# An attention, attention and recurrence kernel: the first image loaded ahead of the parameters, extra products at the start, projections of the first image in pairs, and the last image's blocks in another order

## The chip, the cores and the metric

The kernel runs on one core of a Trainium2 chip. A core has TensorE (PE: matrix products, and PEld for its weight loads), VectorE (DVE), ScalarE (ACT), GpSimd (POOL) and SyncE (SP), which here only issues DMAs. The engines run side by side, each taking its own instructions in order, and wait for each other through semaphores. The metric is the device time of one execution in microseconds; less is better.

## The reference

The input is x, four images of 128 channels and 64 x 64 = 4096 positions, in fp32. Two layers follow.

```
# layer 0, per image
g   = group_norm(x, 32 groups)
vg  = sigmoid(conv_bn(g, Wvg, svg, bvg));  v, gate = split(vg)
q   = conv_bn(g, Wq, sq, bq) * 64 ** -0.5          # 64 x 4096
k   = conv_bn(g, Wk, sk, bk)                        # 64 x 4096
o   = v @ softmax(q.T @ k).T * gate                 # 128 x 4096
x   = x + conv_bn(o, Wp, sp, bp)
# layer 1, per image, t = x as 4096 tokens of 128
h   = layer_norm(t);  qt = h @ W;  t = t + softmax(qt @ qt.T) @ h
# then over all images
wx  = batch_norm(layer_norm(t) @ Wf.T)
y_n = sigmoid(wx_n + y_(n-1) @ V.T)                 # a scan over the tokens
out = t + y
```

conv_bn is a product with a 1 x 1 weight, then a scale and a bias per channel.

## The kernel before, in words

**Sizes.** An image's 4096 positions are eight blocks of 512 (`QB`). An fp32 product shows in the trace as two TensorE instructions; products whose operands have 64 rows run two at a time in the upper and lower half of the array.

**Layer 0** (`attention`, lines 184 to 240, with the callbacks of `layer0`). For each query block n it steps through 16 steps p. A step makes two 64-row score products (L223), one exponential on ScalarE over 1024 columns (L225), an addition on VectorE that collects the softmax's denominators (L230, L232), and, two steps late, the products with the values (L403). After each step one piece of other work is taken from the queue `ahead` or, when that is empty, from `pending`.

**Projections** (`prepare`, lines 289 to 386). The image lies in one tile `xg`. It is loaded in four pieces on SP's queue (L303). `stats` takes the statistics of 512 columns at a time (L307); `mean` and `variance` aggregate (L310) and average over groups with two tiny products (L312, L322), and `inv_sqrt` (L131, L132) runs on GpSimd. `normalise` (L328) works in place. `queries_keys` (L335) makes q and k of 512 positions, moved out of PSUM by VectorE (L339), ScalarE (L343, the copy of q for the lower half of the array) and VectorE again (L347). `values` (L355) makes four value tiles, followed by L360, a tanh on ScalarE (L364) and L365, which together are the sigmoid. `gate` (L370) makes the gate in the same way (L371, L374) and writes it over the normalised image. `chunks` holds four lists, each of two normalisings, two `queries_keys` and two `values`, for chunk i and chunk i + 4; step p of the first query block needs the keys of chunk p // 4 and of that plus four.

For the first image, the statistics, the norm and the first list run before the attention starts (L732); the three other lists and eight gates go into `ahead` (L735), and `need` (L739) takes more of them out when a step needs its keys. For later images all this lies in `ahead` during the layer 1 of the image before.

**Residuals.** When a query block is done, `finish` loads its piece of x (L419), adds a bias on GpSimd (L420) and puts `sums`, `denominators`, `projection` and `tokens` on `pending`. `move` (L257) turns a tile: a 32 x 32 transpose on VectorE (L261), a store to DRAM (L264) and four loads back (L266).

**Layer 1** (`layer1`, lines 475 to 716). Its scores are symmetric, so block n is multiplied only with blocks a from n down to 0; in the order 6, 7, 5, 4, ... 0. Each pair (n, a) is two steps of scores (L672) and exponentials (L678). The products with h (L539, `direct`) come two steps late. For a < n the exponentials are also turned (L683, then 16 DMAs, L710), and `reversed_products` (L552) gives block a its part. `quarter` (L500) saves part of the diagonal pair. `count` finishes a block when it has all its parts: `finish` puts `tokens` (the division, L604 to L610, and a layer norm), `result`, `turn` and `inputs` (L635 to L639) on `pending`. For the last image the pair (1, 0) isn't turned; instead block 0 makes the pair (0, 1) itself, after (0, 0).

**The end.** Batch norm's gain and bias are made (L791 to L796), six dummy products put the banks in order (L787), and 43 steps of the scan follow (L823, L827), each with a sigmoid on ScalarE. Sigmoid isn't in the table that serves Exp and Tanh here. Ahead of that, a sigmoid of one column (L764) is written, whose result no one reads.

**What sets the order.** The program is written as one long list, and a planner then gives each engine its order: it takes what its own estimates show as ready, earlier in the list first. So work can run long before its place in the list: the sigmoid of L764, near the end of the list, runs at 7.3 us. `tc.keep_in_program_order` keeps an instruction at its place.

**The start.** Weights (`w`, 512 KB), per-channel columns (`par`), and four rows repeated over all partitions (`bc`) are loaded on ScalarE's queue (L73 to L81). VectorE multiplies the value and output weights by two of these rows (L122, L123) and halves two columns (L127). Masks are made on GpSimd and VectorE.

## Time and profile before

| | us |
|---|---|
| median of 4 runs (lowest to highest) | 3069.51 (3068.19 to 3070.48) |
| the profiled execution | 3068.22 |
| its span in the trace | 3066.5 |
| first statistics (L307) start | 6.28 |
| group statistics aggregated (L310) from | 15.37 |
| first normalising (L328) | 18.81 |
| first exponential (L225) | 30.12 |
| TensorE without a pause from | 31.2 |
| last product of the attention (L539) ends | 2965.0 |
| last input of the scan (L639) done | 2978.1 |
| scan's last sigmoids (L827) end | 3040.3 |

The trace is of one execution. Busy time is time in which an engine ran an instruction; a busy TensorE isn't always at full clock, and the granted clock is given by stretches (1.00 is full, 0.50 half). Until the first closing that it records the trace shows 1.00, so at the start the clock is read from the instructions' lengths. The chain of waits follows the work back from the last instruction: each piece is what the next one waited for. An instruction's line (L335) is its line in the kernel before.

### The profile page before, as it was taken

The page shows a single profiled execution, that of the slowest core. Times are in us where ns is not written, and L with a number is a line of the kernel's source. Part 1 is how long each engine was busy: PE and PEld are TensorE (multiplying, and loading weights), DVE is VectorE, ACT ScalarE, POOL GpSimd, SP SyncE. Part 2 cuts the span into 40 slices and gives each one's busy share as a digit, 9 for nine tenths or more (in the row PEclk, how much of TensorE's full clock was granted, in tenths as well). Part 3 has the DMA queues.
Part 4 walks back from the last instruction along what each step waited for, and adds up shares of the span by engine and source line. Part 5 has one row for each costly group of instructions (what it writes and reads, how often), then busy time and mean ns, then how long its engine had stood idle before and what let it go on. Part 6 is the DMA issues. An engine that isn't in the chain of part 4 may idle for free.

```text
span 3066.5 us, 32642 instructions
## 1 busy us (share of the span) xinstructions
PE 2999.6 (98%) x10834; PEld 1377.9 (45%) x10834; DVE 1881.1 (61%) x3160; ACT 1154.3 (38%) x2148; POOL 148.6 (5%) x187
## 2 busy tenths in 40 slices
PE   7999999999999999999999999999999999999995
PEld 3444444444444444444444444444444444444443
DVE  6666666655666666655566666655566666455556
ACT  3444433333344443333344443333333444323334
POOL 0000000000000000000000000000000000000000
PEclk9999999999999999999999999999999999999998
DMA  1011143433111123333311113333321112543333
GB/s 52 28 56 56 42 115 86 99 92 93 52 56 55 42 79 97 93 96 91 84 48 60 40 49 109 90 96 93 94 61 56 42 50 93 138 102 92 99 113 157
DMA packets 233171, 241.17 MB, mean 79 GB/s; under 512 B 88480, under 2 KB 144288, under 8 KB 231968
## 3 DMA queue, kind: packets, MB, share of 16 engines
q1 hardware_dynamic: 231984, 238.18, 27.8%
q8 instruction: 89, 1.46, 0.2%
q10 hardware_dynamic: 1008, 0.79, 0.1%
q14 instruction: 90, 0.74, 0.1%
HBM read 65.80 MB, written 56.62 MB: 40 GB/s over the span
## 4 chain that ended last, share of the span: by engine, by line
PE 95%; DVE 3%; ACT 1%; POOL 0%; DMA 0%; issue 0%; ACTq 0%; SPq 0%; DVEq 0%; POOLq 0%
PE o L403 29%; PE o L539 16%; PE ps L223 15%; PE ps L672 14%; PE ot L552 12%; PE m L252 1%; PE m L635 1%; PE mq L497 1%; PE ps L505 1%; PE mp L335 1%; PE mp L370 1%; PE mp L355 1%; DVE t2s L837 1%; DVE ps_r L810 1%; PE m L630 1%; PE m L608 0%
## 5 line engine op out<-in xcount | busy, mean ns | idle before, releaser
L403 PE MATMUL o<-e,nxt 64*128 64x512 f32 x4096 | 964.4, 589 | 0.0
L225 ACT ACTIVATE e<-ps 128x1024 f32<-128x1024 f32 x512 | 521.6, 1025 | 678.0 <-PE ps L223 653.4
L232 DVE TENSOR_TENSOR acc<-acc,e 128x1024 f32<-128x1024 f32 x448 | 548.1, 1223 | 236.8 <-ACT e L225 221.1
L403 PEld LDWEIGHTS o<-e,nxt 64*128 64x128 f32 x4096 | 399.3, 187 | 483.2 <-issue 475.4
L678 ACT ACTIVATE e<-ps,shift 128x512 f32<-128x512 f32 x516 | 350.4, 683 | 670.4 <-PE ps L672 506.1
L539 PE MATMUL o<-e,h 128*128 128x512 f32 x1160 | 539.5, 592 | 0.0
L223 PE MATMUL ps<-nxt 64*128 64x512 f32 x2048 | 536.2, 597 | 2.2 <-ACT e L225 2.2
L672 PE MATMUL ps<-qt 128*128 128x512 f32 x1032 | 490.9, 595 | 2.9 <-ACT qt L498 2.7
L552 PE MATMUL ot<-tt,h 128*128 128x512 f32 x888 | 399.6, 593 | 0.2 <-issue 0.2
L683 DVE STREAM_TRANSPOSE dd<-e 128x512 f32<-128x512 f32 x444 | 286.9, 687 | 85.7 <-ACT e L678 80.2
L539 PEld LDWEIGHTS o<-e,h 128*128 128x128 f32 x1160 | 218.3, 190 | 266.4 <-issue 261.9
L223 PEld LDWEIGHTS ps<-nxt 64*128 64x128 f32 x2048 | 194.5, 187 | 231.4 <-issue 158.6
L672 PEld LDWEIGHTS ps<-qt 128*128 128x128 f32 x1032 | 187.9, 190 | 213.0 <-issue 188.0
L552 PEld LDWEIGHTS ot<-tt,h 128*128 128x128 f32 x888 | 167.9, 190 | 210.0 <-issue 207.3
L557 DVE TENSOR_REDUCE slots<-tt 128x4 f32<-128x2048 f32 x111 | 250.7, 2259 | 8.8 <-DMA tt<-dd 8.2
L566 DVE TENSOR_TENSOR oacc<-oacc,ot 128x512 f32<-128x512 f32 x87 | 59.6, 685 | 188.2 <-PE ot L552 188.1
L131 POOL TENSOR_SCALAR rstd<-mv 128x4 f32<-128x4 f32 x64 | 14.6, 228 | 2432.0 <-DVE mv L277 2432.0
L678 ACT ACTIVATION_READ_ACCUMULATOR e<-ps,shift 128x1 f32 x516 | 101.2, 196 | 0.0
L457 DVE SCALAR_TENSOR_TENSOR t<-yt,rinv,t 128x128 f32<-128x128 f32 x128 | 36.6, 347 | 72.9 <-DMA yt<-turn_d 68.0
L420 POOL TENSOR_SCALAR xb<-xb,bpc 128x512 f32<-128x512 f32 x32 | 61.1, 1909 | 320.2 <-DMA xb<-in_x_dram 320.2
L132 POOL TENSOR_TENSOR rstd<-rstd,mhalf 128x4 f32<-128x4 f32 x64 | 66.4, 1038 | 5.3
L280 DVE TENSOR_SCALAR h<-t,mv,rstd 128x128 f32<-128x128 f32 x128 | 35.7, 342 | 47.1 <-POOL rstd L132 47.1
(160 smaller groups left out, 1657.6 us busy)
## 6 DMA issues: line engine op xcount, KB each, us to landing
tt<-dd SPq DMA_DIRECT2D x1776, 64.0 KB, 2.0
turn_d<-d SPq DMA_DIRECT2D x96, 256.0 KB, 2.0
t_d<-t SPq DMA_DIRECT2D x63, 256.0 KB, 2.0
nxt<-in_x_dram SPq DMA_DIRECT2D x16, 512.0 KB, 6.1
xb<-in_x_dram SPq DMA_DIRECT2D x32, 256.0 KB, 2.9
t<-turn_d SPq DMA_DIRECT2D x128, 64.0 KB, 2.0
yt<-turn_d SPq DMA_DIRECT2D x128, 64.0 KB, 2.0
qt<-turn_d SPq DMA_DIRECT2D x128, 64.0 KB, 2.1
```

Of the source, the lines that this page charges most:

```text
L132: nc.gpsimd.tensor_tensor(dst, dst, mhalf[:, :n], ALU.pow)
L223: nc.tensor.matmul(ps[:, h, :], lhsT=lhsT, rhs=rhs, start=True, stop=True)
L225: nc.scalar.activation(e, ps, AF.Exp, scale=scale)
L232: nc.vector.tensor_tensor(acc, acc, e, ALU.add)
L403: nc.tensor.matmul(o[r], lhsT=v[rs, p + h * PAIRS, :], rhs=e[rs, h, :], start=(p == 0 and h == 0), stop=(p == PAIRS - 1 and h == 1),)
L420: nc.gpsimd.tensor_scalar(xb, xb, bpc, None, ALU.add)
L539: nc.tensor.matmul(o, lhsT=h[:, NQ * a + 2 * i + half, :], rhs=e[:, half, :], start=(a == order(n)[0] and i == 0 and half == 0), stop=(a = ...
L552: nc.tensor.matmul(ot, lhsT=h[:, NQ * n + j, :], rhs=t[:, :, j, :, :].rearrange("q p k j -> q k p j"), start=(j == 0), stop=(j == NQ - 1),)
L557: nc.vector.tensor_reduce(slots[:, bass.ts(n, NQ), a], t.rearrange("q p b k j -> q b p (k j)"), AX.XY, ALU.add,)
L672: nc.tensor.matmul(ps[:, half, :], lhsT=qt[:, bass.ts(at, P)], rhs=qt[:, bass.ts(n, QB)], start=True, stop=True,)
L678: nc.scalar.activation(e[:, half, :], ps[:, half, :], AF.Exp, bias=shift, accum_out=slots[:, at, n : n + 1],)
L683: nc.vector.transpose(d.rearrange("q f b k j -> q k b f j")[:, 2 * i + half], e[:, half, :].rearrange("q (b f j) -> q b f j", b=NQ, f=NQ),)
```

## The change

- The loads of weights and rows move from ScalarE's queue to SP's, into a function `load` that is called after the first image's loads are issued; the rows' order changes. The first image is loaded in eight pieces instead of four.
- The scalings of L122, L123 and L127 move into `scales`, called after the group norm of the first image.
- `warm` makes products that no one reads: three of 512 columns ahead of the statistics, and one of 256 columns each after `mean` and `variance`.
- For the first image, each `queries_keys` and the `values` of the same chunk become one piece of work, and so do two gates; gates alternate between two PSUM pools. `need` counts four pieces a chunk instead of six.
- The first turn (L261) and the sigmoid of L764 are kept at their place in the list, and so are the extra products.
- In the last image's layer 1, block 0 makes the pair (0, 1) first and (0, 0) after; block 1 counts one part more, which it gets when the exponentials of (0, 1) are written.

```diff
--- before.py
+++ after.py
@@ -70,15 +70,20 @@
     wx_d = dram.tile([B, C, N], F32, name="wx_d")
 
     w = const.tile([P, 8 * P], F32, name="w")
-    nc.scalar.dma_start(w, wts)
     w_q, w_k, w_v, w_g, w_p, w_a, w_f, v_t = (w[:, bass.ts(i, P)] for i in range(8))
     par = const.tile([P, 8], F32, name="par")
-    nc.scalar.dma_start(par, cols)
     bpc = const.tile([P, 1], F32, name="bpc")
-    nc.scalar.dma_start(bpc, rows[3:4, :].rearrange("a p -> p a"))
     bc = const.tile([P, 4, P], F32, name="bc")
-    for i in range(4):
-        nc.scalar.dma_start(bc[:, i, :], rows[i, :].partition_broadcast(P))
+
+    def load():
+
+        nc.sync.dma_start(w, wts)
+        nc.sync.dma_start(par, cols)
+        for i in (0, 1):
+            nc.sync.dma_start(bc[:, i, :], rows[i, :].partition_broadcast(P))
+        nc.sync.dma_start(bpc, rows[3:4, :].rearrange("a p -> p a"))
+        for i in (2, 3):
+            nc.sync.dma_start(bc[:, i, :], rows[i, :].partition_broadcast(P))
 
     def col(i):
         return par[:, i : i + 1]
@@ -118,13 +123,15 @@
     nc.gpsimd.memset(ones, 1.0)
     shift = const.tile([P, 1], F32, name="shift")
     nc.gpsimd.memset(shift, -SHIFT)
-
-    nc.vector.tensor_mul(w_v, w_v, bc[:, 0, :])
-    nc.vector.tensor_mul(w_p, w_p, bc[:, 2, :])
     w_vs, w_ps = w_v, w_p
-
     par2 = const.tile([P, 2], F32, name="par2")
-    nc.vector.tensor_scalar(par2, par[:, SG : BG + 1], 0.5, None, ALU.mult)
+
+    def scales():
+
+        nc.vector.tensor_mul(w_v, w_v, bc[:, 0, :])
+        nc.vector.tensor_mul(w_p, w_p, bc[:, 2, :])
+
+        nc.vector.tensor_scalar(par2, par[:, SG : BG + 1], 0.5, None, ALU.mult)
 
     def inv_sqrt(dst, var, eps):
         n = dst.shape[1]
@@ -136,6 +143,7 @@
         tc, x, out, t_d, t2_d, wxs_d, turn_d,
         dict(qk=w[:, DQ : DQ + P], vs=w_vs, g=w_g, ps=w_ps, a=w_a, f=w_f, vt=v_t),
         col, par, par2, bpc, bc, ident, gavg, quart, own, shift, inv_sqrt, par_ok,
+        load, scales,
     )
 
 
@@ -157,7 +165,7 @@
 
 def fast(
     tc, x, out, t_d, t2_d, wxs_d, turn_d, wt, col, par, par2, bpc, bc, ident, gavg, quart,
-    own, shift, inv_sqrt, par_ok,
+    own, shift, inv_sqrt, par_ok, load, scales,
 ):
     nc = tc.nc
     keep_ctx = ExitStack()
@@ -258,7 +266,9 @@
 
             nonlocal n_moves
             d = work.tile([P, 4, NQ, 32], F32, tag="d", name="d", bufs=2)
-            nc.vector.transpose(d.rearrange("q a j i -> q j a i"), blocks)
+            turned = nc.vector.transpose(d.rearrange("q a j i -> q j a i"), blocks)
+            if n_moves == 0:
+                tc.keep_in_program_order(turned)
             via = turn_d[n_moves % len(turn_d)]
             n_moves += 1
             nc.sync.dma_start(via, d)
@@ -289,6 +299,13 @@
         def quarters(t):
             return [t[:, j, :].rearrange("q (p i) -> q p i", p=4) for j in range(NQ)]
 
+        def both(first, second):
+            def run():
+                first()
+                second()
+
+            return run
+
         def prepare(b, bank):
 
 
@@ -299,8 +316,10 @@
             mv = stat.tile([P, 2], F32, tag="gmv", name="gmv", bufs=2)
             dev = stat.tile([P, 3], F32, tag="gdev", name="gdev", bufs=2)
             s6 = stat.tile([P, 8, 6], F32, tag="gs6", name="gs6", bufs=1)
-            for i in range(4):
-                nc.sync.dma_start(xg[:, bass.ts(i, N // 4)], x[b, :, bass.ts(i, N // 4)])
+            pieces = 8 if b == 0 else 4
+            for i in range(pieces):
+                cs = bass.ts(i, N // pieces)
+                nc.sync.dma_start(xg[:, cs], x[b, :, cs])
 
             def stats(i):
                 for j in range(2 * i, 2 * i + 2):
@@ -366,7 +385,7 @@
 
             def gate(ch):
                 cs = bass.ts(ch, 512)
-                m = bank(True)
+                m = bank(ch % 2 == 0)
                 nc.tensor.matmul(m, lhsT=wt["g"], rhs=xg[:, cs], start=True, stop=True)
                 nc.scalar.activation(
                     xg[:, cs], m, AF.Tanh, bias=par2[:, 1:2], scale=par2[:, 0:1]
@@ -383,6 +402,10 @@
                     + [partial(values, c) for c in pair]
                 )
             gates = [partial(gate, c) for c in range(8)]
+            if b == 0:
+
+                chunks[1:] = [[*c[:2], both(c[2], c[4]), both(c[3], c[5])] for c in chunks[1:]]
+                gates = [both(*gates[i : i + 2]) for i in range(0, 8, 2)]
             return (xg, q, k, v), norm, chunks, gates
 
         def layer0(b, gate, q, k, v, need):
@@ -528,7 +551,7 @@
             def order(n):
 
 
-                return [0, 1] if b == B - 1 and n == 0 else list(range(n, -1, -1))
+                return [1, 0] if b == B - 1 and n == 0 else list(range(n, -1, -1))
 
             def turns(n, a):
                 return a < n and not (b == B - 1 and n == 1)
@@ -573,7 +596,7 @@
 
 
                 parts[n] += 1
-                if parts[n] == NB - (b == B - 1 and n < 2):
+                if parts[n] == NB - (b == B - 1 and n == 0):
                     finish(n)
 
             def finish(n):
@@ -696,8 +719,10 @@
                         clock += 1
                         if len(fifo) > LAG:
                             direct()
-                            if a == n and i == 0:
+                            if a == order(n)[0] and i == 0:
                                 direct()
+                        if a > n and i == 1:
+                            count(a)
                         if turned and turned[0][0] <= clock:
                             reversed_products()
                         if pending:
@@ -729,7 +754,26 @@
             return own_bank(spare)
 
         parts0, norm, chunks, gates = prepare(0, first_bank)
-        for work_ in norm + chunks[0]:
+        load()
+
+        def warm(cols):
+
+            m = ps_o.tile([P, QB], F32, tag="o", name="warm")
+            tc.keep_in_program_order(
+                nc.tensor.matmul(
+                    m[:, :cols], lhsT=ident, rhs=parts0[0][:, :cols], start=True, stop=True
+                )
+            )
+
+        for _ in range(3):
+            warm(QB)
+        for work_ in norm[:-2]:
+            work_()
+        for work_ in norm[-2:]:
+            work_()
+            warm(QB // 2)
+        scales()
+        for work_ in chunks[0]:
             work_()
         started.append(True)
         ahead.extend(sum(chunks[1:], []) + gates)
@@ -739,7 +783,7 @@
         def need(n, p):
 
             if n == 0:
-                while p // 4 > 0 and n_ahead - len(ahead) < 6 * (p // 4):
+                while p // 4 > 0 and n_ahead - len(ahead) < 4 * (p // 4):
                     ahead.popleft()()
 
         for b in range(B):
@@ -761,7 +805,7 @@
         flush()
 
 
-        nc.scalar.activation(first_y, shift, AF.Sigmoid)
+        tc.keep_in_program_order(nc.scalar.activation(first_y, shift, AF.Sigmoid))
         ok = big.tile([P, 2, 2 * B * NT], F32, tag="oacc", name="ok")
         nc.vector.tensor_scalar(ok[:, 0, :], den_all, DEN_LO, None, ALU.is_ge)
         nc.vector.tensor_scalar(ok[:, 1, :], den_all, DEN_HI, None, ALU.is_le)
```

## The prediction, made before the result was known

> **What bounds the kernel now.** First the page: TensorE is busy nearly throughout, so the long middle is worth nothing to an edit that removes no TensorE work. Only a place where TensorE stands still, runs at half clock, or pays for switching can give time back.
>
> ```profile
> PE 2999.6 (98%) x10834; PEld 1377.9 (45%) x10834; DVE 1881.1 (61%) x3160; ACT 1154.3 (38%) x2148; POOL 148.6 (5%) x187
> ```
>
> Second, the chain of waits of the start (start, length, what). The reader is to see that the first image's group norm is reached only at 15.37, by way of a residual block (`xb`), its bias add and its turn (L261), which the planner hoisted from work due 60 us later; that the first projections (L335) take 0.94 us an instruction; that a table load stands right before the first exponential; and that the next scores (L223 x4) take 2.08 us.
>
> ```profile
> 8.34 4.56 DMA xb<-in_x_dram
> 12.99 1.64 POOL xb L420
> 14.66 0.71 DVE d L261
> 15.37 0.26 DVE gmv L310
> ...
> 18.81 0.56 DVE nxt L328
> 19.41 3.78 PE pp L335 x4
> 23.19 1.36 PE po L355 x8
> ...
> 28.18 0.63 ACT nxt L364
> 28.83 1.28 ACT L225
> 30.12 1.03 ACT e L225
> 31.20 2.08 PE ps L223 x4
> ```
>
> Third, the image's loads (L303): the first image in two stretches, then the second image, which has the queues to itself. Three loads go out at 0.8 to 1.7 us, but the fourth only at 8.0, and lands 4.3 later, at 12.3. The second image's four go out within 1.4 us, and the last lands by 397.4 + 6.8 = 404.2, 8.1 us after the first issue.
>
> ```profile
> L303 SPq DMA_DIRECT2D nxt<-in_x_dram x3: 393/427/432, 0.8 to 1.7; - x3
> L303 SPq DMA_DIRECT2D nxt<-in_x_dram x1: 328/328/328, 8.0 to 8.0; - x1
> L303 SPq DMA_DIRECT2D nxt<-in_x_dram x4: 351/430/431, 396.1 to 397.4; - x4
> DMA to landing us min/median/max: 4.1/5.4/6.8
> ```
>
> Fourth, the clock, in a table by stretches (length, busy time of PE, PEld, DVE, ACT and POOL, granted clock, DMA). TensorE was idle from 28.99 to 31.20, and the gate closed at about 30.7 for 3.5 us.
>
> ```profile
> 31.00:31.50 0.50, 0.30 (x2) 0.30 (x4) 0.00 (x0) 0.50 (x2) 0.00 (x0) 0.50 0.00 0
> ```
>
> Fifth, the chain of the first query block and of the end. A gate product (L370) costs 1.05 for two instructions and the four score instructions after it 1.06, where undisturbed ones take 0.86 each: 0.39 for going from half-height to full-height weights and back. At the end, the last block's sum (L566) waits behind the layer norm (L280) of the block before it.
>
> ```profile
> 76.65 1.05 PE po L370 x2
> 77.70 1.06 PE ps L223 x4
> 78.76 1.72 PE o L403 x8
> ...
> 2964.24 1.05 POOL rstd L132
> 2965.32 0.04 DVE h L280
> 2965.36 0.22 issue
> 2965.58 0.85 DVE h L280 x3
> 2966.43 0.61 DVE oacc L566
> ```
>
> **The change, part by part.**
>
> (1) **Image first, parameters behind it on SP, first turn held back.** With ACT issuing nothing, I take the second image's pace: last piece at 0.8 + 8.1 = 8.9, one L307 (0.68) to 9.6. Eight pieces instead of four let the statistics run along (8 x 0.6 = 4.8 us of VectorE, begun near 4.2). Aggregation starts at 9.6 instead of 15.37: -5.7. Worst: the last piece lands at 12.3 as now, statistics done at 13.0, -2.4; best, nearer to the 7.5 of the third load now: -6.3. The chain L310 to L328 (3.5 us) is unchanged, so normalising starts near 13.1. SP now issues eight loads and seven parameter loads: 15 x 0.43 = 6.5 us, during which data flow, so w (512 KB at 1.33 us by the second image's pace) lands near 10.2 and the four `bc` rows by about 12.5. In `scales` the product of w_p with the third of them may stand on VectorE ahead of the normalising, and all the projections wait behind it; cover is the 3.5 us of the group norm's chain. `bc` lands up to 7.4 us after issue now; issued at 6.4 that is 13.8: cost 0.7; each further us costs one. I take 0.2. The residual block, queued on SP behind the parameters, isn't needed before the first block ends. The held turn (0.71) then runs on VectorE, which is busy 44.3 of 76 us in the first block. Sum -5.5.
>
> (2) **Extra products.** Three of 512 columns are six instructions, cold 0.94 each: 5.7 us from the first piece's landing (about 4.2) to 9.9, when the mean's product is due at 10.0; uncovered they would cost up to 0.3. The two half ones stand in gaps of the group-norm chain. Gain, if the first projections run warm: the four L335 take 1.7 instead of 3.78 and L355 0.89 instead of 1.36, but VectorE is busy normalising meanwhile and waited for PE only 0.23 (L339) and 0.54 (L360): at most 0.8. Is the gate still open at 13.7? The stretch from 27.3 to 30.7 held 1.7 us of products, and the gate closed. Between 10 and 13.4 the extra and group-norm products come to about 1.1 us. The Trainium skill (TensorE: Matmul & The Clock Gate, Part 1) says that it takes about an idle window of 3.4 us to close it; by that, no gap here is long enough and the gain is 0.8. By this trace, where it closed 1.7 us after the last product, it can be 0. I take -0.5 (0 to -0.8).
>
> (3) **Sigmoid pinned at the end.** Now the planner runs it at 7.3, so the first tanh uses its table and Exp needs another at 28.83. Pinned, the first load serves Identity, Tanh and Exp, as the one at L225 does for all later images. It moves before the first Identity (L343), where ACT has idled 14 us; L347 waits for that only if late: L343 x2 would end at 25.9, L347's second starts at 26.15. Gain 1.28; 0 if the first load is of a set without Exp. The Trainium skill (ScalarE: Activation LUTs, What ACT_TABLE_LOAD costs) adds a drain of about 1.4 us; then it were -2.7. The trace shows 28.81 end of tanh, load to 30.11, Exp at 30.12: no drain. At the end, the new load lies in ACT's 6.3 us of idling before L820, whose own load goes; but L787 keeps PE until 2983.57 and L820 is done at 2983.3, so nothing is gained there. -1.0.
>
> (4) **The second closing of the gate.** With Exp 1.3 us or more earlier, TensorE's gap of 2.2 shrinks to about 0.9. Closed, it cost 2.08 - 1.06 on L223 and 2.26 - 1.72 on L403: 1.56. I take -1.0 (0 to -1.6).
>
> (5) **Pairs.** From 34 to 110 us TensorE is busy all 76; at undisturbed pace its instructions (78 L223 and 160 L403 at 0.215, 16 L370 and 10 L335 at 0.43, 48 L355 at 0.11) make 67.7. Of the 8.3 lost, eight gates at 0.39 are 3.1, and three chunks the rest, 1.6 to 1.8 each, partly because a value product gets between the two halves of a score. After: four gate pairs 1.56, six projection pairs 2.34 at best: -4.4. But the keys are now due right after their pair: L335's end to L347's end took 54.93 to 57.63, 2.7 us, with only 0.9 of value products to cover it. If the two score halves part there again, 0.6 a chunk: -2.6, which I take. If TensorE waits 0.8 for each as well and the chunks stay as dear as now, +0.8. The alternating bank lets two gates stand without waiting for ACT.
>
> (6) **Order and count of the last image.** The second-to-last block can be finished when its scores are through, two steps earlier. Its layer norm then no longer holds L566 (o was ready at 2965.0, L566 ran at 2966.43) nor puts L636 (0.7) before the last L277: -2.3 at best. But its products L621, L630, L635 (1.7 us) now go before TensorE's last one, less 0.5 of idle: +1.3 against it. I take -0.9 (-2.3 to +0.8).
>
> Sum: -5.5 -0.5 -1.0 -1.0 -2.6 -0.9 = -11.5. The profiled execution took 3068.2 (span 3066.5 and 1.7 around it); less 11.5 is 3056.7. The median shown is 3069.5, 1.3 above it: **3058.0**.
>
> **Rivals.** *Only the loads count* (0.18): the gate closes in between, keys stall the pairs, the end trades evenly. (1) and half of (3), -6.1: 3063.4, on the edge of what can be told from no change. For it: the 2.2 us gap that closed the gate. Against it: the gates' 3.1 is plain switching, and halves without any help.
>
> *All of it* (0.14): every term at its best, -6.3 -0.8 -1.3 -1.6 -4.4 -2.3 = -16.7: 3052.8. It needs the gate open through the group norm, against the row at 30.7.
>
> *Slower* (0.06): the paired lumps starve TensorE. Where two projections' followers stand before an exponential on ACT and VectorE, TensorE waited 2.2 us and then lost 1.56 to the clock, as at 28.99: 3.7 in all. There are ten lumps. The other terms give 8.9, so it is slower from three lumps on, measurably so from five; with six, +22.2 - 8.9 = +13.3: 3082.8. Against it: a lump with its score step asks ACT for 0.77 + 0.63 + 1.02 = 2.4 us and VectorE for 4.0, against some 4.7 of TensorE; and from 34 to 110 no wait stopped TensorE.
>
> **How the numbers follow.** The likeliest (0.62) gives 3058.0, itself within 3054.5 to 3062. The range, 3053.0 to 3064.5, takes in both neighbours and leaves out the slower case and the edges. What this kernel's measurement can tell from no change is about 0.2%, 6.1 us: below 3063.4. Faster: 0.62 + 0.14 + half of 0.18 = 0.85; same 0.09; slower 0.06.
>
> **What would show it.** (1): L310 at 9 to 10 us and the first L328 near 13; no parameter wait on VectorE. (2): L335 at about 0.45 an instruction. (3): two table loads, none between tanh and Exp. (4): no half clock after the first Exp. (5): gates in twos; the second query block finished some 10.6 us earlier than now. (6): L604 of the second-to-last block well before 2961 less the shift. It is wrong if the parameters land after 14, if the table or the gate keep their places, or if the planner deals the middle anew: it orders all engines by its own estimates, and no row tells how it answers.

## The result, and the profile after

| | before | after |
|---|---|---|
| median, us (lowest to highest) | 3069.20 (3065.76 to 3072.09), 60 runs | 3063.48 (3061.42 to 3065.55), 40 runs |
| ratio, 95% interval | | 0.9983 (0.9979 to 0.9987) |
| the profiled execution, its span | 3068.22, 3066.5 | 3061.41, 3059.6 |

The change makes the kernel faster by 5.7 us, half of the 11.5 predicted and some 5.5 above the predicted median. The time lies in the range, near its upper end, and the gain of 0.17% lies on the edge named as resolvable; its 95% interval lies clear of no change. From here on an L number is a line of the changed kernel: L322 is the old L303, L347 L328, L354 L335, L374 L355, L231 L223, L233 L225, L426 L403, L443 L420, L389 L370, L562 L539, L831 L787.

TensorE's row of the page is what it was: the middle is full, and the time went at the edges.

```profile
PE 3003.4 (98%) x10844; PEld 1380.7 (45%) x10844; DVE 1881.4 (61%) x3160; ACT 1153.2 (38%) x2147; POOL 147.9 (5%) x187
```

The chain of waits of the start and of the first image's projections (start, length, what). To see: the image's last piece is in by 9.48 (4.07 + 5.41), where before loads held the chain till 12.90; yet GpSimd's residual add (L443) still stands on the chain, now *inside* the group norm; no table load is left before the first exponential, and the next scores take 1.13 instead of 2.08; further on, after two projections' work, score and value products come in single halves (0.50, 0.42); and two gates (L389) share one switch of weights.

```profile
4.07 5.41 DMA nxt<-in_x_dram
9.49 4.12 DMA xb<-in_x_dram
13.78 1.59 POOL xb L443
15.37 0.56 POOL gdev L139
15.95 0.56 DVE nxt L347
16.55 3.71 PE pp L354 x4
20.26 0.91 PE po L374 x8
...
25.85 1.03 ACT e L233
26.92 1.13 PE ps L231 x4
...
34.69 0.89 PE po L374 x8
35.58 1.05 PE ps L231 x2
36.63 0.86 PE o L426 x2
37.49 0.50 PE ps L231
38.00 0.42 PE ps L231
...
72.79 1.05 PE po L389 x2
73.84 0.86 PE mp L389 x2
74.70 1.06 PE ps L231 x4
```

The image's loads in the first 6 us: eight issues without a stall, where the fourth piece was issued only at 8.0 before.

```profile
L322 SPq DMA_DIRECT2D nxt<-in_x_dram x8: 392/432/432, 0.8 to 4.1; - x8
```

GpSimd's instructions from 9 to 20 us. The reciprocal root of the group norm is L138 and L139; the add stands between them, and L139 starts at 15.34, 1.76 after the end of L138.

```profile
13.35 0.23 POOL L138 TENSOR_SCALAR gdev<-gdev 128x1 f32<-128x1 f32 x1 [10.71 <-DVE gdev L342]
13.78 1.59 POOL L443 TENSOR_SCALAR xb<-xb,bpc 128x512 f32<-128x512 f32 x1 [0.20 <-DMA xb<-in_x_dram]
15.34 0.58 POOL L139 TENSOR_TENSOR gdev<-gdev,mhalf 128x1 f32<-128x1 f32 x1
```

The clock by stretches (the columns of the table shown before). The extra products did not keep the gate open: the clock is at half from 13.2 (the row from 13.00 to 13.50 has 0.73) and still at 19.0 to 19.5, while the first projections run. After the first exponential it stays open.

```profile
13.50:14.00 0.50, 0.35 (x1) 0.00 (x0) 0.00 (x0) 0.00 (x0) 0.30 (x2) 0.50 0.00 0
19.00:19.50 0.50, 0.50 (x2) 0.23 (x1) 0.47 (x1) 0.00 (x0) 0.00 (x0) 0.50 0.00 0
26.50:27.00 0.50, 0.24 (x3) 0.08 (x2) 0.50 (x2) 0.47 (x2) 0.00 (x0) 1.00 0.00 0
```

So the two traces differ as follows (the aggregation is taken from its own start, 15.29 before; the chain's piece of it begins at 15.37). Of the experiments below, five leave the start as it is in the changed kernel (e_chunks, e_gates, e_tailold, e_tailbank, e_tailfront); with it they make six profiles of one start, whose mean stands in the last column.

| stretch | before | after | difference | mean of six |
|---|---|---|---|---|
| to the aggregation (L310, now L329) | 15.29 | 10.83 | -4.46 | -4.03 |
| aggregation to first normalising | 3.52 | 5.12 | +1.60 | +1.68 |
| first normalising to first exponential | 11.31 | 9.90 | -1.41 | -0.72 |
| first exponential to the end of the first eight value products | 5.42 | 3.92 | -1.50 | -1.50 |
| from there to the first gate (three chunks) | 41.11 | 43.02 | +1.91 | |
| first gate to the copy of the second block | 64.40 | 62.80 | -1.60 | |
| copy of the last image's last block in layer 0 to the dummies (L831) | 385.18 | 385.27 | +0.09 | |

From the second block to that copy every block shows the same shift of 5.4 to 5.5: nothing is won or lost between. At the dummies the two traces stand 5.4 apart. The spans differ by 6.9 because from the first dummy to the end the kernel before takes 88.3 and the changed one 86.8; the twelve other runs, with the changed kernel's scan (in e_sigfree with its table load as before), take 86.7 to 87.8 there. Part of that goes with the phase of the clock gate, which is closed when the dummies begin: it opens 5.2 after the first dummy in the kernel before and 3.2 in the changed one, and the later it opens in a run, the later the scan's last sigmoid ends (61.0 after the first dummy in e_chunks, where it opens at 2.9, 62.1 in e_tailbank, where it opens at 5.3). So the median's 5.7, and not the spans' 6.9, is the measure of the change.

### The profile page after: what moved, and what is told of

Same layout as the page of the kernel before. It is cut to its first block, busy times and chain, and to the rows that moved or that the text cites. A ratio compares the mean times of both kernels' runs of the same rounds, so it can differ in the third digit from the quotient of the medians.

```text
span 3059.6 us, 32664 instructions
## 1 busy us (share of the span) xinstructions
PE 3003.4 (98%) x10844; PEld 1380.7 (45%) x10844; DVE 1881.4 (61%) x3160; ACT 1153.2 (38%) x2147; POOL 147.9 (5%) x187
## 4 chain that ended last, share of the span: by engine, by line
PE 95%; DVE 3%; ACT 1%; POOL 0%; issue 0%; DMA 0%; SPq 0%; DVEq 0%; POOLq 0%; ACTq 0%
PE o L426 29%; PE o L562 16%; PE ps L231 15%; PE ps L695 14%; PE ot L575 12%; PE m L260 1%; PE m L658 1%; PE mq L520 1%; PE ps L528 1%; PE mp L389 1%; PE mp L354 1%; PE mp L374 1%; DVE t2s L881 1%; DVE ps_r L854 1%; PE m L653 1%; PE m L631 0%
## 5 line engine op out<-in xcount | busy, mean ns | idle before, releaser
L426 PE MATMUL o<-e,nxt 64*128 64x512 f32 x4096 | 966.2, 589 | 0.0
L233 ACT ACTIVATE e<-ps 128x1024 f32<-128x1024 f32 x512 | 521.5, 1025 | 684.5 <-PE ps L231 664.4
L426 PEld LDWEIGHTS o<-e,nxt 64*128 64x128 f32 x4096 | 400.1, 187 | 483.1 <-issue 474.2
L562 PE MATMUL o<-e,h 128*128 128x512 f32 x1160 | 539.5, 592 | 0.0
L231 PE MATMUL ps<-nxt 64*128 64x512 f32 x2048 | 535.2, 596 | 1.2 <-DVE nxt L366 0.9
L562 PEld LDWEIGHTS o<-e,h 128*128 128x128 f32 x1160 | 218.2, 190 | 265.8 <-issue 261.0
L231 PEld LDWEIGHTS ps<-nxt 64*128 64x128 f32 x2048 | 194.2, 187 | 228.8 <-issue 151.3
L589 DVE TENSOR_TENSOR oacc<-oacc,ot 128x512 f32<-128x512 f32 x87 | 59.6, 685 | 187.9 <-PE ot L575 187.8
L138 POOL TENSOR_SCALAR rstd<-mv 128x4 f32<-128x4 f32 x64 | 14.6, 228 | 2352.0 <-DVE mv L287 2352.0
L443 POOL TENSOR_SCALAR xb<-xb,bpc 128x512 f32<-128x512 f32 x32 | 60.4, 1887 | 386.8 <-DMA xb<-in_x_dram 363.9
L139 POOL TENSOR_TENSOR rstd<-rstd,mhalf 128x4 f32<-128x4 f32 x64 | 66.4, 1038 | 5.3
L290 DVE TENSOR_SCALAR h<-t,mv,rstd 128x128 f32<-128x128 f32 x128 | 35.7, 342 | 47.2 <-POOL rstd L139 47.2
```

The lines of the kernel that those rows point to most:

```text
L139: nc.gpsimd.tensor_tensor(dst, dst, mhalf[:, :n], ALU.pow)
L231: nc.tensor.matmul(ps[:, h, :], lhsT=lhsT, rhs=rhs, start=True, stop=True)
L233: nc.scalar.activation(e, ps, AF.Exp, scale=scale)
L426: nc.tensor.matmul(o[r], lhsT=v[rs, p + h * PAIRS, :], rhs=e[rs, h, :], start=(p == 0 and h == 0), stop=(p == PAIRS - 1 and h == 1),)
L443: nc.gpsimd.tensor_scalar(xb, xb, bpc, None, ALU.add)
L562: nc.tensor.matmul(o, lhsT=h[:, NQ * a + 2 * i + half, :], rhs=e[:, half, :], start=(a == order(n)[0] and i == 0 and half == 0), stop=(a = ...
```

## The experiments

Each kernel is the changed one with one edit. The table gives the median, its ratio to the kernel before, the time from the start to the end of the first eight value products, from there to the second block's copy, and the last stretch of the table above. A ratio's interval is 0.0007 to 0.0014 to either side, 2 to 4 us, so neighbouring medians are told apart mostly by the stretches; the time to the second copy repeats within 0.05 where the code in it is the same, the last stretch only within 1.5 (384.7 to 386.2).

| kernel | median | ratio | first eight products end | to second copy | end |
|---|---|---|---|---|---|
| before | 3069.20 | 1 | 35.54 | 105.51 | 385.18 |
| changed | 3063.48 | 0.9983 | 29.77 (mean of six 30.97) | 105.82 | 385.27 |
| e_loadact | 3066.52 | 0.9993 | 33.62 | 105.82 | 386.06 |
| e_addlate | 3063.80 | 0.9983 | 30.46 | 105.81 | 384.74 |
| e_defer | 3062.64 | 0.9981 | 29.55 | 105.82 | 386.15 |
| e_nowarm | 3062.09 | 0.9979 | 29.89 | 105.83 | 385.02 |
| e_hold | 3060.07 | 0.9975 | 28.48 | 105.82 | 385.54 |
| e_sigfree | 3065.33 | 0.9991 | 32.85 | 105.78 | 385.01 |
| e_chunks | 3061.47 | 0.9976 | 30.89 | 103.92 | 384.86 |
| e_gates | 3065.65 | 0.9990 | 31.64 | 107.42 | 384.91 |
| e_tailold | 3063.12 | 0.9981 | 31.12 | 105.82 | 384.66 |
| e_tailbank | 3063.50 | 0.9982 | 30.83 | 105.82 | 384.73 |
| e_tailfront | 3060.33 | 0.9975 | 31.56 | 105.82 | 382.42 |
| e_best | 3055.36 | 0.9957 | 28.26 | 103.92 | 381.62 |

My theory after reading the two traces: the early image brings its 4 us, but draws GpSimd's residual add into the group norm; pairs of gates save the switch, pairs of projections lose more than they save; the end is held by TensorE's list. The rivals: the loads themselves are worth less than they look; the extra products, not the add, set the start; a bank holds the end.

### The loads: e_loadact

```diff
-        nc.sync.dma_start(w, wts)          # and the other six
+        nc.scalar.dma_start(w, wts)        # and the other six
-        parts0, norm, chunks, gates = prepare(0, first_bank)
         load()
+        parts0, norm, chunks, gates = prepare(0, first_bank)
-            pieces = 8 if b == 0 else 4
+            pieces = 4
```

> Undoes the loading part alone: parameters on ScalarE's queue ahead of the image, which comes in four pieces. If the arrival is worth what the trace says (aggregation 15.29 to 10.83) and the chain behind it keeps the length that it has in the changed kernel, aggregation comes back to 14 to 15 and the median rises by 3 to 4.5, to 3066.5 to 3068. If the residual's add was the price of the early image alone and leaves the chain again (3.5 in place of 5.1), the rise is 2 to 3: 3065.5 to 3066.5. If another thing than the loads sets the start, no change (3063.5).

Aggregation came at 14.80, and the median rose by 3.0; the first eight products ended 2.65 after the mean of six. GpSimd's rows from 9 to 20 us:

```profile
13.34 1.57 POOL L443 TENSOR_SCALAR xb<-xb,bpc 128x512 f32<-128x512 f32 x1 [10.70 <-DMA xb<-in_x_dram]
17.44 0.23 POOL L138 TENSOR_SCALAR gdev<-gdev 128x1 f32<-128x1 f32 x1 [2.53 <-DVE gdev L342]
```

With the image late, the add is over before the root begins, and aggregation to normalising takes 3.57 again. So the loads are worth about 3 (3.0 by the median, 2.65 by the stretch), after the add's 1.6 to 1.8 has been paid. That price comes with the early image: the root now falls where the add always ran. It isn't the early image's alone, though: without the extra products (e_nowarm, below) the add stands behind the root as well.

### The residual's add: e_addlate and e_defer

```diff
-                nc.gpsimd.tensor_scalar(xb, xb, bpc, None, ALU.add)
+                added = nc.gpsimd.tensor_scalar(xb, xb, bpc, None, ALU.add)
+                if b == 0 and n == 0:
+                    tc.keep_in_program_order(added)
```

> The changed kernel with one edit: the first residual block's bias add on GpSimd is kept at its place in the list, so it can't stand between the two steps of the reciprocal root. If the add is what held the first normalising (15.37 - 13.58 = 1.8 us in the profile after), L347 starts near 14.2 instead of 15.95 and the second query block finishes about 1.8 us earlier than in the changed kernel, near 133.8; time about 3061.7. If the wait was something else (the parameters on VectorE, or the weights behind the image), L347 stays within 0.4 of 15.9 and so does the rest. The closed clock gate could also eat part of it: the first projections would then take as long or longer, and the second block would gain less than 1 us.

The median did not move (3063.80). The add did leave the root: normalising started 3.81 after the aggregation. But it then ran beside it (14.94 to 16.53), and the first two normalisings (L347) took 926 and 980 ns; the longest of all 32 in the changed kernel takes 546. The first projection started 5.69 after the aggregation, in the changed kernel 5.72.

```profile
L347 DVE TENSOR_SCALAR nxt<-nxt,gdev x1: 980/980/980, 15.8 to 15.8; 128x512 f32<-128x512 f32 x1
```

Hence the second form, which makes the block's load wait for the first image's keys, by a one-column copy into its tile, so that the add comes after the start:

```diff
+                if b == 0 and n == 0:
+                    nc.gpsimd.tensor_copy(xb[:, 0:1], k[:, N // 2 - 1 : N // 2])
                 nc.sync.dma_start(xb, x[b, :, cs])
                 nc.gpsimd.tensor_scalar(xb, xb, bpc, None, ALU.add)
```

> The changed kernel with the first residual block's load made to wait for the last keys of the first image (about 70 us), by a copy of one column on GpSimd, so that its bias add falls neither between the steps of the reciprocal root nor beside the normalising. If GpSimd's add and VectorE's normalising slow each other when side by side (with the add moved only behind the root, the first two normalisings took 0.93 and 0.98 us instead of 0.54, and the second began 0.8 after the first), L347 starts 3.8 us after the aggregation, each takes 0.54 and the first projection follows 0.6 after the first; the first exponential comes 1.0 to 1.8 us earlier than in the changed kernel, against the aggregation. If the two slow normalisings had another cause (the row products, the port being taken by the loads), they stay slow.

Normalising started 3.41 after the aggregation, none of the 32 took more than 547 ns, and the first eight products ended 1.4 before the mean of six, though only 0.2 before the quickest of the six. The median went down by 0.8 only, within its interval. Of the 1.7 that the chain lost, 1.4 by the stretch and 0.8 by the median came back, neither of them clear of chance. The first projection now waited for the second normalising too (1.06 after the first one instead of 0.60), and the gate was closed till 20.5.

### The extra products: e_nowarm and e_hold

```diff
-        for _ in range(3):
-            warm(QB)
...
             work_()
-            warm(QB // 2)
```

> The changed kernel without the extra products. If they hold the clock for the first projections' followers and the first scores, the second query block finishes 0.5 to 2 us later than in the changed kernel, with half clock during L374 or after the first exponential. If they do nothing for the time (in the profile after the gate had closed again at 13.6, ahead of the first projections), it finishes within 0.5; and as the bias add no longer stands inside the reciprocal root in this order, 1.8 us earlier, near 133.8, which would make the extra products the cause of that loss.

Without them the kernel was not slower: 3062.09, and the first eight products ended 1.1 before the mean of six. Their going changed the planner's order: the add stood behind the root, as in e_addlate, and normalising started 3.57 after the aggregation. The pace was hardly worse: L354's four took 3.78 and L374's sixteen 3.13, but in the five other profiles of the changed start they took 3.78 and 2.37 to 3.15 too; only the changed kernel's own was quicker, with 0.91 for the first eight of L374. So as written the extra products bring nothing that can be told from none.

e_hold is e_defer with more of them: five of 512 columns ahead, and two more after the variance, which read the last piece of the image (`warm` gets a second argument for that, left out here).

```diff
-        for _ in range(3):
+        for _ in range(5):
             warm(QB)
...
             warm(QB // 2)
+        for _ in range(2):
+            warm(QB, N - QB)
```

> The run before with more extra products: five of 512 columns ahead of the mean instead of three, and two more of 512 after the variance, which read the last piece of the image, so that TensorE is busy from the first piece on up to the first projection. If what closes the gate is a window that isn't full of products, the first four projections take 1.7 to 2.0 us instead of 3.7, whatever the phase, and the first exponential comes some 1 us earlier than without (VectorE then bounds it). If the products at full clock are too thin for the gate, or VectorE bounds all of it, the gain is under 0.4.

3060.07; the first projections started 1.2 later than in e_defer, behind the added products, but took 2.22 instead of 3.78, and the first eight products ended 1.1 earlier. The gate still closed, at about 14.2, but opened again at 17.5, after TensorE had been busy with the added products and the first projections without a pause; in e_defer, where it stood still between 14.2 and 15.7, it opened only at 20.5. The clock in e_hold:

```profile
14.20:14.70 0.50, 0.50 (x2) 0.34 (x1) 0.04 (x1) 0.00 (x0) 0.43 (x1) 0.50 0.00 0
17.50:18.00 0.50, 0.50 (x2) 0.19 (x1) 0.00 (x0) 0.00 (x0) 0.00 (x0) 0.93 0.00 0
```

### The sigmoid's table: e_sigfree

```diff
-        tc.keep_in_program_order(nc.scalar.activation(first_y, shift, AF.Sigmoid))
+        nc.scalar.activation(first_y, shift, AF.Sigmoid)
```

> The changed kernel with the sigmoid of the end not held at its place. If the table load it causes ahead of the first exponential was worth 1.3 us and the closing of the gate behind it another 1.5, the first exponential comes 1.3 us later than in the changed kernel, the next scores (L231 x4) take 2 us instead of 1.1, and the second query block finishes up to 2.8 us later. If the gate stays open anyway, it is 1.3 only. If the load is hidden beside TensorE's scores, nothing.

The table load returned to the chain of waits, and with it the second closing of the gate (the clock is 0.65 in the half us from 28.0 and 0.50 in the next):

```profile
26.14 1.28 ACT L233
27.44 1.03 ACT e L233
28.51 2.08 PE ps L231 x4
30.59 2.26 PE o L426 x8
```

Median +1.85, first eight products 1.9 after the mean of six. So one pinned instruction is worth about 1.9: it removes the load, and through it the 2.2 us pause that closed the gate.

### The pairs: e_chunks and e_gates

```diff
-                chunks[1:] = [[*c[:2], both(c[2], c[4]), both(c[3], c[5])] for c in chunks[1:]]
...
-                while p // 4 > 0 and n_ahead - len(ahead) < 4 * (p // 4):
+                while p // 4 > 0 and n_ahead - len(ahead) < 6 * (p // 4):
```

> The changed kernel with the three projection lists of the first image taken apart again (six pieces a list, six counted by need), gates still in twos. If paired projections cost time (the three lists took 43.0 us after against 41.1 before), the second query block finishes 1.9 us earlier than in the changed kernel; time about 3061.6. If pairing them is worth what it saves in switches and the loss came from elsewhere (the second load of the banks, the start), it finishes the same or later, by up to 2.6.

```diff
-                gates = [both(*gates[i : i + 2]) for i in range(0, 8, 2)]
```

> Undoes the pairs of gates alone; the projections stay paired. If the pairs save the switch between half-height and full-height weights, the eight gates cost 1.6 more: first sum to the second block's copy 108.4 (changed kernel 106.8), median 3065.1. If the saving has another source (the alternating bank, which stays), 106.8 and 3063.5.

Undoing each alone moved its own stretch, and both came out as expected: single projections bring the three chunks from 43.02 back to 41.11, single gates the rest from 62.80 back to 64.40, each to the value of before. The chain of waits of e_gates shows a switch for each gate, where the changed kernel's has two gates in one:

```profile
74.66 1.06 PE po L389 x2
75.71 1.06 PE ps L231 x4
...
78.49 1.06 PE mp L389 x2
```

What the rows show of the paired projections' loss: VectorE's and ScalarE's instructions of the changed kernel around 35 us, and the keys (L366) of a single projection in e_chunks.

```profile
34.78 0.80 DVE L358 TENSOR_SCALAR nxt<-mp,par 64x512 f32<-64x512 f32 x1
35.62 0.69 DVE L379 TENSOR_TENSOR nxt<-po,bc 128x512 f32<-128x512 f32 x1
35.61 0.77 ACT L362 ACTIVATE nxt<-mp,par 64x512 f32<-64x512 f32 x1 [2.01 <-DVE nxt L358]
36.42 0.82 DVE L366 TENSOR_SCALAR nxt<-mp,par 64x512 f32<-64x512 f32 x1
```

```profile
48.22 0.82 DVE L366 TENSOR_SCALAR nxt<-mp,par 64x512 f32<-64x512 f32 x1 [0.84 <-ACT nxt L362]
```

The pair's work is over on TensorE at 35.58, but the keys for the lower half (L366) come only at 37.2. They come last in a row of three moves out of the same bank: VectorE's L358, ScalarE's L362, VectorE's L366. The values' move (L379), which the pair put with them, runs while L366 waits for L362, so it is not what makes the keys late; in e_chunks they follow their projection (46.53, 49.03) as late, by 2.5 (here from 34.7 to 37.2). What differs is TensorE's work in that time. From 35.58 TensorE takes the one half of the score that it has, then value products, and the halves of scores and of value products go on parted until 43.57. In e_chunks they part as well, but there the second `values` (L374, 1.09) stands after the first score half, where the changed kernel has value products that part.

That the keys are late in both forms is in the rows; that the parted value products make up the 0.64 a chunk is argued, not tried.

### The end: e_tailold, e_tailbank, e_tailfront

```diff
-                return [1, 0] if b == B - 1 and n == 0 else list(range(n, -1, -1))
+                return [0, 1] if b == B - 1 and n == 0 else list(range(n, -1, -1))
-                if parts[n] == NB - (b == B - 1 and n == 0):
+                if parts[n] == NB - (b == B - 1 and n < 2):
-                            if a == order(n)[0] and i == 0:
+                            if a == n and i == 0:
-                        if a > n and i == 1:
-                            count(a)
```

> Undoes the last image's order and count alone. Theory: as changed, the second-to-last block's transposes keep their late place in TensorE's list, so the order is worth nothing: dummies start 385.2 after the copy at 2587 as in the changed kernel, median 3063.5 within 0.5. Rival: the change's order gains at one place and loses at another (its products ahead of TensorE's last one), and undone it moves the end by more than 0.5.

3063.12, and 384.66 for the stretch, where the nine kernels with the changed end have 384.7 to 386.2: the order as changed is worth nothing that can be measured. The chain of waits at the changed kernel's end shows why:

```profile
2954.15 1.72 PE o L562 x4
2955.87 0.45 PE m L631 x4
...
2960.34 0.85 DVE h L290 x3
2961.18 0.61 DVE oacc L589
2961.84 0.66 PE ml L631 x4
```

Block 1 has its denominators by 2950.3, so the new count does its part. But its transposes (L631) run at 2955.87, 5.6 us later, behind products (L562) of the last block. So its layer norm (L290) still stands on VectorE before the last block's sum (L589), as it did before. Two causes were open, a bank and TensorE's place in the list. The first, a bank of its own:

```diff
                     def bank():
+                        if b == B - 1 and n == 1:
+                            return ps_o.tile([P, QB], F32, tag="o", name="m1o")
                         return ps_m.tile([P, QB], F32, tag="m", name="m1")
```

> The changed kernel with the second-to-last block's four pieces given a bank of another PSUM pool. If the single bank shared with the block before is what held its transposes (L631 at 2955.7, right after the copy that frees the bank at 2954.2, where its denominators were ready at 2950.3), its division starts near 2951 and the last block's sum is no longer queued behind its layer norm: the dummy products (L831) start 1 to 2 us earlier against the start of the last stage; time about 3062. If TensorE's own order or the last products bound it, no change within 0.4 us.

3063.50, the transposes as late as before: not the bank. The second keeps that bank and puts block 1's tokens at the head of `pending`, which gives out one piece a step:

```diff
+                elif b == B - 1 and n == 1:
+                    pending.appendleft(tokens)
+                    pending.extend([result, turn, inputs])
                 elif b == B - 1 and n < 4:
```

> The changed kernel with the second-to-last block's first piece put at the head of the pending work (two steps earlier) and with a bank of its own. With the bank alone its transposes stayed where they were, behind the four products L562 of the step before, so if TensorE's place in the list is what binds, they now start 3 to 5 us earlier, the last block's sum is no longer queued behind that block's layer norm, and the dummy products start 1 to 2 us earlier against the end of the layer 0 of the last image (385.3 us from its last block to the dummies in the changed kernel). If the last products of TensorE bind, the 1.7 us of its own products moved ahead of them cancel this: within 0.5.

3060.33, and the stretch is 382.42, 2.85 less. Its chain of waits:

```profile
2948.49 0.44 PE m1o L633 x4
...
2956.68 3.43 PE o L562 x8
2960.11 0.44 PE m1o L646 x4
2960.55 0.44 PE m1o L655 x4
2960.99 0.58 PE ml L633 x4
```

The transposes run at 2948.49 and block 1's layer norm is out of the way; TensorE goes from its last product to the last block's own transposes with only 0.88 of block 1's work between. So the place in the list held the end, and a bank of its own was not enough. Whether the place alone would do is open: it was tried only together with the bank, and in the changed kernel the shared bank is in use by the block before (L653, L658) for much of the time from 2949.3 to 2954.

### Together: e_best

Single projections, paired gates, the deferred add with more extra products, and the end of e_tailfront.

> The changed kernel with the three repairs that the earlier runs point to: first image's projections single again, the residual's bias add held out of the head with more extra products, and block 1's tokens at the head of the pending work in a bank of its own. If the three gains are independent, they add: -1.9 (projections), -1.3 to -3.4 (head, by the median of the run with more extra products), -2.9 (end), so 3063.5 less 6.1 to 8.2: 3055.3 to 3057.4. First block to second block's copy 104.9 after the first sum (changed kernel 106.8); dummies start 382.4 after the copy at 2587 (changed kernel 385.3). If the planner's answer to one repair spoils another, above 3059.

3055.36 (3054.36 to 3056.39, five runs), ratio 0.9957 (0.9944 to 0.9971): faster than the kernel before by 13.8 us and than the changed one by 8.1, the intervals of the two ratios being apart. By the stretches 2.7 of it is the start (28.26 against the mean of six), 1.9 the chunks (103.92), 3.7 the end (381.62). The gains add. In this profile the gate stayed open through the group norm, and the four first projections took 1.98:

```profile
16.50:17.00 0.50, 0.49 (x2) 0.30 (x2) 0.50 (x3) 0.00 (x0) 0.00 (x0) 1.00 0.00 0
```

## Why the prediction was half right

| part | predicted | traces | its worth by undoing it alone, stretch (median) |
|---|---|---|---|
| (1) image first | -5.5 | -2.9 | -2.65 (-3.0) |
| (2) extra products | -0.5 | with (3) -1.4, mean of six -0.7 | +1.1 (+1.4) |
| (3) sigmoid pinned, (4) second closing | -2.0 | (4) -1.5 | -1.9 (-1.9) |
| (5) pairs | -2.6 | +0.3 | gates -1.6 (-2.2), projections +1.9 (+2.0) |
| (6) order and count | -0.9 | +0.1 | +0.6 (+0.4), within chance |
| sum | -11.5 | -5.4 | |

Of the 6.1 between the two sums, 2.6 are (1), 2.9 (5) and 1.0 (6), less 0.4 that (2) to (4) together gave more than said. The last column doesn't sum to the change, since the add's 1.6 to 1.8 is charged to both (1) and (2): undoing either takes it off the chain.

**(1)** The arrival was right in kind and somewhat short: the last piece landed at 9.5 (said 8.9), and the masks' instructions, 0.6 of VectorE, stood between the last statistics, so aggregation came at 10.83 instead of 9.6. The step that failed is "the chain L310 to L328 (3.5 us) is unchanged": it took 5.12. I had read the add at 12.99 to 14.63 as part of what made the old chain late, noted that the load of the block now comes later, and did not ask where the add would then fall: it needs GpSimd at 13.8, when the root does too. The bounds set for the parameters were wide enough: VectorE waited 0.17 for them, and 0.16 to 0.53 in the five other profiles of this start.

**(2)** My middle value lay between two readings, the gate of the trace and the page TensorE: Matmul & The Clock Gate (Part 1) of the Trainium skill, which wants an idle window of 3.4 us for a closing. The trace was the better guide: from 9.82 to 13.23 TensorE was busy for 1.44 of 3.41, and at 13.23 the gate closed. What I left out is that five more products change the planner's order for the other instructions.

**(3), (4)** Right together, 2.0 said and 1.9 found when undone. As expected there was no drain beside the load's 1.28. But the second closing was worth all of its 1.5, not the 1.0 taken, which leaves 0.4 for the table load instead of 1.0 (0.7 by the stretch from normalising to the exponential, 11.3 in e_sigfree against a mean of 10.6): that the two errors cancelled in the sum is luck.

**(5)** Gates: 1.56 said, 1.60 found. Projections: "if the two score halves part there again, 0.6 a chunk" was the step. The mechanism was the one named, but its term was too small: against the pace of undisturbed halves, three chunks lost 5.2 before, 2.34 is the switching left in pairs, and 7.1 is lost now; so the parted halves take 4.8, 1.6 a chunk. (The 5.2 is the prediction's own estimate. The rows say about the same: after a chunk's second pair TensorE takes 9.70 from 35.58 for 12 score and 24 value instructions, which make 7.74 at 0.215 each, 1.96 more, some 0.2 of it the switch.) The +0.8 kept as the worst end, from 0.8 of waiting for each of the keys, was the nearer one.

**(6)** "Its layer norm then no longer holds L566" failed: a block that is counted earlier is not done earlier while its first TensorE instruction keeps its turn. A gain of that size was there to be had, by another edit: e_tailfront got 2.85. (The terms of the -2.3 come to 1.43 + 0.7 = 2.1, and those against it to 1.2.)

The rival *Only the loads count* gave 3063.4, and the time came out there, but not by its way: the loads, 5.5 there, gave 2.9 with the add's loss; table, clock and gate pairs, 0.6 there, gave 4.5; and the paired projections, nothing there, took 1.9 back. A total that agrees is no proof of a mechanism. The slower rival didn't occur: no lump stopped TensorE.

## What to carry to other kernels

When a chain is made to start earlier, lay its instructions on each engine beside what already runs at the new time, above all on the slow ones: here one GpSimd instruction of 1.6 us off the path moved onto it by standing still. Pairing saved the switch here where the results were due late (gates, 1.6), and lost more than it saved where the next step needed them (keys, 1.9): pair the first kind, leave the second single. And where an order is written as a list, a condition met earlier is worth nothing until the first instruction that it frees is also placed earlier (here it had a bank of its own, too).

## What the runs showed of the hardware

- VectorE's normalising of 128 x 512 (L347) takes 0.53 to 0.55, but 0.78 to 0.98 while GpSimd's add runs (e_addlate, e_nowarm; two of the kernel before, 0.82 and 0.92, beside its add of 2.02 at 19.09). The Trainium skill (SBUF — State Buffer, Who interferes with whom) has the two engines share a pair of ports in VectorE's two-port modes, the later one blocked for a whole instruction. In which mode the normalising ran no trace shows, but it wasn't blocked so: in e_addlate it began 0.04 after the add, was slowed to 0.93 and ended at 15.90, before the add did at 16.53.
- The clock at the start differs between executions of the same code: in the six profiles of one start L354 took 3.71 to 3.78 in all, but from the first of them to the first scores (L231) it was 7.29 to 8.35, and from the aggregation to the end of the eighth product 18.94 to 20.17. The gate was closed for 6.8 in the changed kernel's own profile (13.2 to 20.1) and for 10.2 in the five others (12.4 to 22.6 in e_tailbank), which fits its being the quickest. So one profile of a start carries about 1 us of chance, more than most terms of the prediction; of the kernel before there is only one.
